# Final rows stored into the output and added to by scatters, a place per tile, VectorE roots and per-tile first weights in a routed transformer layer

## The chip, the cores and the metric

The kernel runs on one core of one Trainium2 chip. The metric is the device time of one execution in microseconds (us). Engines are named as the profile names them: PE (matmul), PEld (its weight loads), DVE (VectorE), ACT (ScalarE), POOL (GpSimd), SP (SyncE, which here only issues DMAs).

## The reference

x is 4 x 1024 x 256 in float32, 4096 tokens in all. LN is the layer norm without scale over the 256 channels.

```python
x = x + attention(LN(x)) @ w_proj.T     # causal, ALiBi slopes, 16 heads of 16
u = LN(x)
# attention over the first axis: each of the 1024 positions attends over the batch of 4
a = attention_over_batch(u @ in_proj_w.T + in_proj_b) @ out_w.T + out_b
h = LN(u + a) * ln1_g + ln1_b
probs = softmax(h @ router_w.T + router_b)          # 8 experts
assign = max(top_k(probs, 2).indices)               # the larger index of the best two
moe = gelu(h @ w1[assign].T + b1[assign]) @ w2[assign].T + b2[assign]
out = x + LN(h + moe) * ln2_g + ln2_b
```

Each token goes through one expert, number 1 to 7 (the larger of two different indices is never 0).

## The kernel before, in words

`kernel` lays the weights out and launches `tile_layer` (L2470), which runs `fast_layer` (L607 to 2467) and, under a flag that is not set here, a general fallback `general_layer` (L93). PE, DVE and ACT are called through a helper that records what they are given (`Watched`, L579), so in the profile nearly all their instructions stand at line 589 and are told apart by the names of their tiles. POOL and SP show their own lines.

The work comes in these stages:

- **Causal attention** in rounds of `score` and `weigh` (L986 to 1070), whose probabilities are masked by POOL (L1017). It fills some 600 us.
- **Fronts.** `front(i)` (L1593 to 1855) takes block i of 128 positions with all 4 of the batch, 512 tokens. It normalises x into u, projects q, k, v (`qkvp`), does the 4-way attention on DVE (`pr`, `sc`, `pv`), turns the result round with PE (`turned_sum`, L1724), projects, normalises h, and scores the router. Two rows per token are then stored by SP in one DRAM table `rows` of 4096 x 512: h normalised but not yet scaled (`rows<-u`, L1787 on) and x + ln2_b (`rows<-x`, `store_later`, L1613). There are 8 fronts; the earlier ones run inside the attention, the last one in the tail beside the first tiles.
- **Tables.** A tile is 128 tokens of one expert. `tabulate_first` (L1299) sorts the tokens of the first 6 fronts into 18 tiles (0_0 to 0_17), `tabulate_rest` (L1346) those left over and the last two fronts into 20 tiles (1_0 on). For each tile they find which rows to gather (`rows_`), where in the output they belong (`out_rows`), the expert's offset into the weights (`at_w`) and its one-hot row (`chosen`). The last 4 of the 20 run only under a condition that is not met here, so 34 tiles run.
- **Tiles** (class `Tile`, L1858). `gather` (L1865): POOL fetches 128 rows of 512 by an indirect DMA into a buffer `given`. `stages` (L1905): PE transposes h (`mtp`); ACT scales it by ln1 into `mt`; PE makes `hid` = w1 x mt + b1; ACT takes gelu (`ge`); PE sums `oe` = b2 + h (a matmul of `mt` with the identity) + w2 x ge. In the profile w1 and w2 are both `w`.
- **Pairs of tiles** are finished together by `finish_tiles` (L1961): DVE takes mean and variance from `oe`, POOL the root by a power (`norm_root`, L827, `rstd_v`), DVE makes (oe - mean) x ln2_g and then x rstd + (x + ln2_b) into `o` (4 buffers), and POOL scatters `o` into the output by an indirect DMA (`out_dram`, L1983) after a small memset (L1982).

w1 of all seven experts is loaded into SBUF by SP at the start of the tail (`load_layer`), and w2 a little later (`of_late`). The first 4 tiles load their own w1 and w2 (`load_weights`, L1874). For all others ACT copies the expert's w1 out of the resident one into one of 3 buffers (`copy_w1`, L1891), because its offset is a register's value; w2 is read in place.

**What sets the order.** Each engine takes its instructions in program order, and that order is written by a planner in Python. Generators such as `front` yield the engine and the cost of their next part (`yield "E", 2.0` is 2.0 us of DVE); the loop at L2417 takes whichever can begin first, and puts a tile's step (`tile_step`, L2415) in where PE would be free. A tile's costs are in `TILE` (L71). `Experts` (L1993) holds the tiles in flight: `fetch` takes a new one if one of the 18 `given` buffers is free (the pair that held it is finished), `advance` moves each tile in flight a stage on. 5 tiles of the first table are held back (`HELD_BACK`) to be issued around and after the second table. After `tabulate_rest`, `late["wide"]` is set: from there on only tiles are left, and `oe` has more buffers. The check of the attention's sums (`check_sums`, L2366) goes in at the eighth step after that, and its flag decides on the fallback.

Of the kernel before, what the change touches and what calls it, by code (L numbers as in the profile page):

```python
# [58 lines left out]
STEEP = -400.0  # L59
MASKED = -1e30  # L60
# [4 lines left out]
EARLY = 0  # L65
N_OWN = 4
N_GIVEN = 18
N_W1 = 3
HELD_BACK = 5

TILE = (("PE", 2.6), ("DVE", 1.7), ("ACT", 1.9), ("POOL", 2.3))  # L71
TILE_HALF, LAG, COPIED, FIRST_BY, W1_THERE, LOAD_W2 = 1.3, 0.2, 1.0, 0.1, 14.0, 2.0
# [535 lines left out]
def fast_layer(ctx: ExitStack, tc: tile.TileContext, odd, x, wq, wk, wv, wp, w_in, w_out, w_r,  # L608
# [222 lines left out]

    def norm_apply(dst, src, n, mv, rstd, name, scalar=False):
# [352 lines left out]
    given = [const(f"given{n}", [P, 2 * C]) for n in range(EARLY)]  # L1185
# [4 lines left out]
    def prepare():  # L1190
        nc.vector.tensor_scalar(lower, mask, -1.0, None, ALU.is_lt)
        nc.vector.memset(ones_bf, 1.0)
        nc.vector.memset(one_e, 1.0)
        for t in b_bf + [in_bf, out_bf]:
            nc.vector.memset(t, 0.0)
        for t in given:
            nc.gpsimd.memset(t, 0.0)

    class Routing:
# [6 lines left out]
        def prepare(self):  # L1206
            self.so_far = const("so_far", [P, E], BF16)
            nc.vector.memset(self.so_far, 0.0)
            self.rows_of = dram.tile([N_COLUMNS * P, 2 * C], F32, tag="rows", name="rows")
# [384 lines left out]
    def front(i, fact, more, last):  # L1594
# [3 lines left out]
        rows_of = part.rows_of.rearrange("(k t p) c -> k p t c", t=B, p=P)[i]  # L1598
        yield "E", 2.5
# [13 lines left out]
        def store_later():  # L1613
            for t in range(B):
                nc.sync.dma_start(rows_of[:, t, C:2 * C], at_x(t))
            left_x[i // PC] += 1
# [101 lines left out]
        if last:  # L1718
# [5 lines left out]
            def turned_sum(t, pr):  # L1724
                pt = bank(f"ctp_{i}_{t}")[:, :C].rearrange("p (c q) -> p c q", q=P)
                for cc in range(CC):
                    for k in range(B // 2):
                        nc.tensor.matmul(
                            pt[:, cc], pr[:, k, cc * P:(cc + 1) * P], ident,
                            start=k == 0, stop=k == B // 2 - 1,  # L1730
# [4 lines left out]
            for t in range(B):  # L1735
                yield "E", 2.0, 1.0 if t else 0.0
# [3 lines left out]
                nc.vector.tensor_tensor(pr[:, 0:2], pr[:, 0:2], pr[:, 2:4], ALU.add)  # L1740
# [49 lines left out]
        store(("u", i), lambda: nc.sync.dma_start(rows_of[:, :, 0:C], u))  # L1790
# [67 lines left out]
    class Tile:  # L1858


        def __init__(self, table, j):
            self.table, self.j, self.name = table, j, f"{table.n}_{j}"
            self.w1 = self.w2 = None
# [10 lines left out]
        def load_weights(self):  # L1874
# [6 lines left out]
            self.w1, self.w2 = (  # L1881
                const(f"{name}_{self.name}", [P, CC, C], into=late["tail"])
                for name in ("w1", "w2")
            )
            for t, src in ((self.w1, w1), (self.w2, w2)):
                nc.sync.dma_start(
                    t.rearrange("p c f -> p (c f)"),
                    src.rearrange("p e c f -> p (e c f)")[:, bass.ds(at + CC * C, CC * C)],
                )

        def copy_w1(self):  # L1891

            at = nc.values_load(
                self.table.at_w[0:1, self.j:self.j + 1], engines=[mybir.EngineType.Activation],
                min_val=0, max_val=(E - 2) * CC * C,
                skip_runtime_bounds_check_because="an expert is 1 to E - 1",
            )
# [63 lines left out]
    def finish_tiles(two):  # L1961

        n, name = len(two), two[0].name
        mv, rstd = norm_stats(lambda k: two[k].v, n, f"v_{name}", "_v")
        norm_root(rstd, n)
        yield
        if experts.waiting():
            yield
        os = []
        for k, t in enumerate(two):  # L1970
            o = late["work"].tile([P, C], F32, tag="o", name=f"o_{t.name}", bufs=4)
            nc.vector.scalar_tensor_tensor(
                o, t.v, mv[:, k, 0:1], row(G2), ALU.subtract, ALU.mult
            )
            nc.vector.scalar_tensor_tensor(
                o, o, rstd[:, k:k + 1], t.hx[:, C:2 * C], ALU.mult, ALU.add
            )
            os.append(o)
        if experts.waiting():
            yield  # L1980
        for t, o in zip(two, os):
# [4 lines left out]
                in_=o, in_offset=None, bounds_check=B * T - 1, oob_is_err=False,  # L1986
# [6 lines left out]
    class Experts:  # L1993
# [559 lines left out]
```

## Time and profile before

| what | value |
|---|---|
| median of 3 runs | 774.32 us (772.24 to 775.04) |
| the profiled execution | 776.72 us |
| its span | 774.9 us |
| granted PE clock, mean | 0.97 |
| PE busy | 696.7 us (90% of the span) |
| DVE, ACT, POOL busy | 514.0, 425.9, 243.0 us |
| gathers (POOL L1868) | 34, 1100 ns each |
| scatters (POOL L1983) | 34, 1018 ns each |
| last PE instruction ends | 759.2 us |

Times in the profile are microseconds from the start of the span; 1.8 us of the execution lie outside it. A row of a timeline gives start, duration, engine, line and operation, then the tiles written <- read with their shapes, how many records are joined (x4), and in brackets how long the engine was idle before it and what ended that. A row of the waits gives engine, tile and line of the waiting instruction <- what released it: the total of idle us, how often, the longest. A row of the stretches gives its window and length, then the busy us of PE, PEld, DVE, ACT and POOL, the granted PE clock, the busy share of the DMA engines and GB/s. An f32 matmul leaves two records, a transpose or a bf16 matmul one. "issue" is idle time for which the profile shows no release.

### The profile page before, as it was taken

What the parts mean: (1) busy time and instruction counts of PE and PEld (TensorE: products, weight loads), DVE (VectorE), ACT (ScalarE), POOL (GpSimd) and SP (SyncE); (2) the same over time, 40 slices, a digit from 0 to 9 for tenths busy, and PEclk for the clock granted to TensorE, in tenths of its full rate; (3) what the DMA queues carried; (4) which work ended last, traced back from release to release, by engine and by line L of the source; (5) the groups of instructions that cost most, each with busy time, mean ns of one, the idle gap of its engine ahead of it and who ended that gap; (6) DMA issues with size and microseconds to landing.
All of it is one profiled execution on the core that took longest, in us unless ns stands there. A gap on an engine that the chain in (4) does not pass through costs nothing. (4 is left out here: it accounts for less than half of the span.)

```text
span 774.9 us, 21884 instructions
## 1 busy us (share of the span) xinstructions
PE 696.7 (90%) x8945; PEld 525.6 (68%) x8945; DVE 514.0 (66%) x1266; ACT 425.9 (55%) x647; POOL 243.0 (31%) x345
## 2 busy tenths in 40 slices
PE   3989899999999999999989999999999687989991
PEld 2667577666666666575668877687778456878891
DVE  5447436477985765899672427698679778877462
ACT  1545547555465656556557656568558054546550
POOL 4644113221222221104221221123112330478873
PEclk9999999999999999999999999999999898999996
DMA  7535544431452432315354445345342670344421
GB/s 227 167 117 176 172 129 139 139 118 49 129 160 86 140 113 67 102 58 159 93 172 134 142 146 164 93 139 187 112 116 58 174 282 1 110 137 128 125 82 41
DMA packets 70872, 98.48 MB, mean 127 GB/s; under 512 B 15408, under 2 KB 54635, under 8 KB 70252
## 3 DMA queue, kind: packets, MB, share of 16 engines
q1 hardware_dynamic: 58528, 67.82, 28.4%
q10 hardware_dynamic: 7884, 16.05, 6.6%
q0 software_dynamic: 4352, 13.11, 5.6%
q8 instruction: 74, 1.21, 0.6%
q14 instruction: 34, 0.28, 0.1%
HBM read 60.50 MB, written 34.59 MB: 123 GB/s over the span
## 5 line engine op out<-in xcount | busy, mean ns | idle before, releaser
L589 ACT ACTIVATE p<-sk 128x1024 f32<-128x1024 f32 (+1 forms) x320 | 287.9, 940 | 148.4 <-PE sk L589 118.6
L1017 POOL TENSOR_SCALAR_AFFINE_SELECT p<-p 128x512 f32<-128x512 f32 (+1 forms) x160 | 106.6, 670 | 404.8 <-ACT p L589 402.5
L589 PE MATMUL sk<-slots 32*128 32x128 f32 (+1 forms) x3456 | 178.5, 325 | 10.1 <-DVE kq L589 4.7
L589 PEld LDWEIGHTS sk<-slots 32*128 32x128 f32 x3456 | 134.6, 187 | 53.5 <-issue 20.5
L589 PE MATMUL pv<-p,v 128*32 128x128 f32 (+1 forms) x3456 | 146.9, 317 | 9.6 <-ACT p L589 4.0
L589 PEld LDWEIGHTS pv<-p,v 128*32 128x32 f32 x3456 | 96.9, 111 | 48.8 <-issue 10.0
L589 PE MATMUL qkvp<-w_in,ut 128*128 128x264 f32 (+1 forms) x240 | 83.5, 486 | 0.2 <-ACT ut L589 0.2
L589 PEld LDWEIGHTS qkvp<-w_in,ut 128*128 128x128 f32 x240 | 42.5, 190 | 28.8 <-issue 24.3
L589 PE MATMUL qkp<-xt,wqk 128*128 128x256 f32 x224 | 56.4, 397 | 0.0
L589 DVE COPY kq<-qkp 128x512 f32<-128x512 f32 x28 | 19.1, 684 | 50.1 <-PE qkp L589 50.1
L589 PEld LDWEIGHTS qkp<-xt,wqk 128*128 128x128 f32 x224 | 41.5, 194 | 10.7 <-issue 3.3
L589 PE MATMUL hid<-mt,w 128*128 128x128 f32 x272 | 41.4, 289 | 2.6 <-ACT ge L589 1.7
L589 ACT ACTIVATE mt<-mtp,columns 128x128 f32<-128x128 f32 x68 | 27.4, 454 | 26.9 <-PE mtp L589 26.9
L589 ACT COPY qkv<-qkvp 128x512 f32<-128x512 f32 x28 | 16.4, 585 | 44.9 <-PE qkvp L589 44.7
L589 DVE TENSOR_TENSOR pv<-vr,sc 128x1024 f32<-128x1024 f32 x32 | 39.2, 1224 | 2.4 <-PE ctp L589 2.1
L1868 POOL DMA_INDIRECT given<-rows,rows x34 | 37.4, 1100 | 9.0 <-issue 7.9
L589 DVE COPY vr<-qkvp 128x264 f32<-128x264 f32 x28 | 12.1, 431 | 42.1 <-PE qkvp L589 42.1
L589 PEld LDWEIGHTS hid<-mt,w 128*128 128x128 f32 x272 | 37.2, 198 | 3.9 <-ACT ge L589 2.2
L589 DVE TENSOR_REDUCE sc<-pr 128x64 f32<-128x1024 f32 x32 | 39.0, 1220 | 1.1
L589 DVE TENSOR_TENSOR pr<-qkv 128x1024 f32<-128x1024 f32 x32 | 39.2, 1224 | 0.5 <-ACT qkv L589 0.2
L1983 POOL DMA_INDIRECT out_dram<-o,out_rows x34 | 34.6, 1018 | 7.4 <-issue 5.0
L589 PE MATMUL oe<-w,ge 128*128 (+1 forms) x136 | 36.8, 395 | 0.0
(320 smaller groups left out, 1005.1 us busy)
## 6 DMA issues: line engine op xcount, KB each, us to landing
slots<-k SPq DMA_DIRECT2D x32, 320.0 KB
k<-kq SPq DMA_DIRECT2D x32, 256.0 KB
v<-v ACTq DMA_DIRECT2D x4, 1152.0 KB
x<-in_x_dram SPq DMA_DIRECT2D x16, 256.0 KB
y<-yt SPq DMA_DIRECT2D x16, 256.0 KB
rows<-x SPq DMA_DIRECT2D x32, 128.0 KB
slots<-k SPq DMA_DIRECT2D x16, 256.0 KB
rows<-u SPq DMA_DIRECT2D x8, 512.0 KB
```

The costliest lines, as they stand in the source:

```text
L589: ins = made(*args, **kwargs)
L1017: nc.gpsimd.affine_select(blocks, blocks, pattern=[[0, 2], [0, size], [1, P]], compare_op=ALU.is_ge, fill=0.0, base=0, channel_multiplier=-1,)
L1868: nc.gpsimd.indirect_dma_start(out=self.hx, out_offset=None, in_=t.rows_of, in_offset=bass.IndirectOffsetOnAxis(ap=t.rows_[:, self.j:self. ...
L1983: ins = nc.gpsimd.indirect_dma_start(out=out.rearrange("t n c -> (t n) c"), out_offset=bass.IndirectOffsetOnAxis(ap=t.table.out_rows[:, t. ...
```

## The change

- Where x + ln2_b was stored into the table, it is stored straight into the output. The table has only h: 4096 x 256, and a gather brings 256 numbers per row.
- The scatters add (`compute_op=ALU.add`) what LN(h + moe) x ln2_g gives to the rows that lie in the output. The product is made in the tile's own gathered row: DVE's (oe - mean) x ln2_g overwrites `given`, ACT scales it there by rstd, and POOL scatters it from there. `o` and the second DVE operation are gone.
- Each tile has a place of its own in `given` (19 pairs); `fetch` no longer waits for a finished one.
- Behind the table (`wide`) the root is taken by DVE: a first guess by integer arithmetic and three Newton steps on 128 x 2 numbers, 12 small operations in `norm_root_v`. Ahead of it POOL still does it.
- w1 is not kept in SBUF. Each tile's w1 (256 KB) comes from DRAM by SP, with the offset in a register of SP, into one of 8 buffers. w2 is loaded first, and always read in place. ACT's copies are gone.
- In `turned_sum` of the last front, PE transposes and sums four parts where DVE first added them to two and PE multiplied two by the identity. In `oe` the identity's product becomes a transpose and comes ahead of the bias.
- The planner's numbers follow: `TILE`, a yield of the last front (2.0 to 1.3), when tiles may begin.

The parts of the diff that matter:

```diff
@@ -57,19 +57,18 @@
 N_LAST = 4
 NOWHERE = 1 << 20
+GUESS = float(0x5F3759DF - 0x00400000)
...
-EARLY = 0
-N_OWN = 4
-N_GIVEN = 18
-N_W1 = 3
+N_AHEAD = 4
+N_W1 = 8
...
-TILE = (("PE", 2.6), ("DVE", 1.7), ("ACT", 1.9), ("POOL", 2.3))
-TILE_HALF, LAG, COPIED, FIRST_BY, W1_THERE, LOAD_W2 = 1.3, 0.2, 1.0, 0.1, 14.0, 2.0
+TILE = (("PE", 2.5), ("DVE", 1.2), ("ACT", 1.7), ("POOL", 2.6))
+TILE_HALF, LAG, COPIED, FIRST_BY, W2_THERE = 1.3, 0.2, 1.0, 0.1, 2.0
...
@@ -829,6 +828,26 @@
+    def norm_root_v(mv, rstd, n):
+        half = small.tile([P, 2], F32, tag="half_v", name="half_v")[:, :n]
+        y = small.tile([P, 2], F32, tag="root_v", name="root_v")[:, :n]
+        by = rstd[:, :n]
+        nc.vector.tensor_scalar(half, mv[:, :n, 1], EPS, 0.5, ALU.add, ALU.mult)
+        nc.vector.tensor_single_scalar(
+            y.bitcast(I32), half.bitcast(I32), 1, op=ALU.logical_shift_right
+        )
+        nc.vector.tensor_scalar(
+            y.bitcast(I32), y.bitcast(I32), -1.0, GUESS, ALU.mult, ALU.add
+        )
+        for k in range(3):
+            nc.vector.tensor_tensor(by, y, y, ALU.mult)
+            nc.vector.scalar_tensor_tensor(by, by, -1.0, half, ALU.mult, ALU.mult)
+            nc.vector.scalar_tensor_tensor(
+                by if k == 2 else y, by, 1.5, y, ALU.add, ALU.mult
+            )
...
@@ -1206,7 +1223,7 @@
-            self.rows_of = dram.tile([N_COLUMNS * P, 2 * C], F32, tag="rows", name="rows")
+            self.rows_of = dram.tile([N_COLUMNS * P, C], F32, tag="rows", name="rows")
...
@@ -1596,6 +1613,8 @@
+
+        out_of = out.rearrange("t (k p) c -> k p t c", p=P)[i]
...
@@ -1612,7 +1631,7 @@
-                nc.sync.dma_start(rows_of[:, t, C:2 * C], at_x(t))
+                nc.sync.dma_start(out_of[:, t], at_x(t))
...
@@ -1723,21 +1742,21 @@
             def turned_sum(t, pr):
                 pt = bank(f"ctp_{i}_{t}")[:, :C].rearrange("p (c q) -> p c q", q=P)
+
                 for cc in range(CC):
-                    for k in range(B // 2):
+                    for k in range(B):
                         nc.tensor.matmul(
                             pt[:, cc], pr[:, k, cc * P:(cc + 1) * P], ident,
-                            start=k == 0, stop=k == B // 2 - 1,
+                            is_transpose=True, start=k == 0, stop=k == B - 1,
                         )
                 nc.scalar.copy(ct[:, :, t * P:(t + 1) * P], pt)
             pr = None
             for t in range(B):
-                yield "E", 2.0, 1.0 if t else 0.0
+                yield "E", 1.3, 1.0 if t else 0.0
                 if t:
                     turned_sum(t - 1, pr)
                 pr = weighted(t)
-                nc.vector.tensor_tensor(pr[:, 0:2], pr[:, 0:2], pr[:, 2:4], ALU.add)
             yield "D", 1.0
             turned_sum(B - 1, pr)
             for t in range(B):
...
@@ -1878,28 +1897,12 @@
                 min_val=0, max_val=(E - 2) * CC * C,
                 skip_runtime_bounds_check_because="an expert is 1 to E - 1",
             )
-            self.w1, self.w2 = (
-                const(f"{name}_{self.name}", [P, CC, C], into=late["tail"])
-                for name in ("w1", "w2")
-            )
-            for t, src in ((self.w1, w1), (self.w2, w2)):
-                nc.sync.dma_start(
-                    t.rearrange("p c f -> p (c f)"),
-                    src.rearrange("p e c f -> p (e c f)")[:, bass.ds(at + CC * C, CC * C)],
-                )
-
-        def copy_w1(self):
-
-            at = nc.values_load(
-                self.table.at_w[0:1, self.j:self.j + 1], engines=[mybir.EngineType.Activation],
-                min_val=0, max_val=(E - 2) * CC * C,
-                skip_runtime_bounds_check_because="an expert is 1 to E - 1",
-            )
             self.w1 = late["work"].tile(
                 [P, CC, C], F32, tag="w1", name=f"w1_{self.name}", bufs=N_W1
             )
-            nc.scalar.copy(
-                self.w1.rearrange("p c f -> p (c f)"), late["w1"][:, bass.ds(at, CC * C)]
+            nc.sync.dma_start(
+                self.w1.rearrange("p c f -> p (c f)"),
+                w1.rearrange("p e c f -> p (e c f)")[:, bass.ds(at + CC * C, CC * C)],
             )
         def stages(self):
...
@@ -1915,15 +1918,12 @@
                     mt[:, cc], pt[:, cc], AF.Identity,
                     bias=columns[:, 1, cc:cc + 1], scale=columns[:, 0, cc:cc + 1],
                 )
-            if not self.w1:
-                self.copy_w1()
             yield
-            if not self.w2:
-                at = nc.values_load(
-                    self.table.at_w[0:1, j:j + 1], engines=[mybir.EngineType.PE],
-                    min_val=0, max_val=(E - 2) * CC * C,
-                    skip_runtime_bounds_check_because="an expert is 1 to E - 1",
-                )
+            at = nc.values_load(
+                self.table.at_w[0:1, j:j + 1], engines=[mybir.EngineType.PE],
+                min_val=0, max_val=(E - 2) * CC * C,
+                skip_runtime_bounds_check_because="an expert is 1 to E - 1",
+            )
...
@@ -1946,44 +1946,48 @@
-            nc.tensor.matmul(self.v, sel, b_bf[1], start=True, stop=False)
+
             for cc in range(CC):
                 nc.tensor.matmul(
-                    self.v[:, cc * P:(cc + 1) * P], mt[:, cc], ident, start=False, stop=False
-                )
+                    self.v[:, cc * P:(cc + 1) * P], mt[:, cc], ident,
+                    is_transpose=True, start=cc == 0, stop=False,
+                )
+            nc.tensor.matmul(self.v, sel, b_bf[1], start=False, stop=False)
             for fc in range(CC):
                 nc.tensor.matmul(
                     self.v, ge[:, fc],
-                    self.w2[:, fc] if self.w2 else late["w2"][:, bass.ds(at + fc * C, C)],
+                    late["w2"][:, bass.ds(at + fc * C, C)],
                     start=False, stop=fc == CC - 1,
                 )
     def finish_tiles(two):
-        n, name = len(two), two[0].name
-        mv, rstd = norm_stats(lambda k: two[k].v, n, f"v_{name}", "_v")
-        norm_root(rstd, n)
+        n = len(two)
+        tiles = norm_tiles(f"v_{two[0].name}", "_v")
+        _, mv, rstd = tiles
+        for k, t in enumerate(two):
+            norm_one(tiles, k, t.v)
+
+            nc.vector.scalar_tensor_tensor(
+                t.hx, t.v, mv[:, k, 0:1], row(G2), ALU.subtract, ALU.mult
+            )
+        if late["wide"]:
+            norm_root_v(mv, rstd, n)
+        else:
+            norm_end(tiles, n)
+            norm_root(rstd, n)
         yield
+        for k, t in enumerate(two):
+            nc.scalar.activation(t.hx, t.hx, AF.Identity, scale=rstd[:, k:k + 1])
         if experts.waiting():
             yield
-        os = []
-        for k, t in enumerate(two):
-            o = late["work"].tile([P, C], F32, tag="o", name=f"o_{t.name}", bufs=4)
-            nc.vector.scalar_tensor_tensor(
-                o, t.v, mv[:, k, 0:1], row(G2), ALU.subtract, ALU.mult
-            )
-            nc.vector.scalar_tensor_tensor(
-                o, o, rstd[:, k:k + 1], t.hx[:, C:2 * C], ALU.mult, ALU.add
-            )
-            os.append(o)
-        if experts.waiting():
-            yield
-        for t, o in zip(two, os):
+        for t in two:
             nc.gpsimd.memset(spare, 0.0)
             ins = nc.gpsimd.indirect_dma_start(
                 out=out.rearrange("t n c -> (t n) c"),
                 out_offset=bass.IndirectOffsetOnAxis(ap=t.table.out_rows[:, t.j:t.j + 1], axis=0),
-                in_=o, in_offset=None, bounds_check=B * T - 1, oob_is_err=False,
+                in_=t.hx, in_offset=None, bounds_check=B * T - 1, oob_is_err=False,
+                compute_op=ALU.add,
             )
             if late["n_out"]:
                 tc.declare_no_dep(ins.ins, group="rows", reason="a token is in one tile")
...
@@ -1996,30 +2000,27 @@
         def __init__(self):
             self.step, self.fetched = 0, []
-            self.n_fetched = self.n_finished = 0
+            self.n_fetched = 0
             self.under_way, self.done, self.finishing = [], [], []
         def fetch(self):
             self.step += 1
-            if tiles_to_do and self.n_fetched - self.n_finished < len(given):
+            if tiles_to_do and given:
                 t = tiles_to_do.pop(0)
-                t.gather(given[self.n_fetched % len(given)])
-                if self.n_fetched < N_OWN:
-                    t.load_weights()
+                t.gather(given[self.n_fetched])
+                t.load_weights()
                 self.n_fetched += 1
                 self.fetched.append((t, self.step))
         def finish(self):
             for it in list(self.finishing):
-                n, stages = it
-                if next(stages, self) is self:
+                if next(it, self) is self:
                     self.finishing.remove(it)
-                    self.n_finished += n
             n = 1 if len(self.done) + len(self.under_way) + self.waiting() < 2 else 2
             if len(self.done) >= n:
                 two, self.done = self.done[:n], self.done[n:]
-                self.finishing.append((len(two), finish_tiles(two)))
-                next(self.finishing[-1][1])
+                self.finishing.append(finish_tiles(two))
+                next(self.finishing[-1])
...
@@ -2037,10 +2038,6 @@
-            if self.fetched and self.n_fetched > 2 * N_OWN + 1:
-                t, _ = self.fetched[0]
-                if not t.w1:
-                    t.copy_w1()
...
@@ -2330,32 +2327,31 @@
     issue_stores(age=0)
-    load_sums(last_unit)
...
-    w1_sb, w2_sb = (const(name, [P, E - 1, CC, C], into=tail) for name in ("w1", "w2"))
-
-    def load_layer(sb, src):
-        for lo, hi in ((1, 3), (3, 5), (5, E)):
-            nc.sync.dma_start(sb[:, lo - 1:hi - 1], src[:, lo:hi])
+    w2_sb = const("w2", [P, E - 1, CC, C], into=tail)
+    for lo, hi in ((1, 3), (3, 5), (5, E)):
+        nc.sync.dma_start(w2_sb[:, lo - 1:hi - 1], w2[:, lo:hi])
     late.update(
         tail=tail, work=work, ps=ps_x, wide=False, n_oe=0, n_out=0, n_hid=0,
-        w1=w1_sb.rearrange("p e c f -> p (e c f)"), w2=w2_sb.rearrange("p e c f -> p (e c f)"),
+        w2=w2_sb.rearrange("p e c f -> p (e c f)"),
     )
-    for k in range(EARLY, N_GIVEN):
-        if k < EARLY + X_BUFS - B - G // 2:
-            given.append(xpool.tile([P, 2 * C], F32, tag="x", name=f"given{k}"))
+
+    for k in range(N_TILES // 2):
+        if k < X_BUFS - B - G // 2:
+            two = xpool.tile([P, 2, C], F32, tag="x", name=f"given{k}")
         else:
-            given.append(const(f"given{k}", [P, 2 * C], into=tail))
-    for _ in range(N_OWN):
+            two = const(f"given{k}", [P, 2, C], into=tail)
+        given += [two[:, 0], two[:, 1]]
+    for _ in range(N_AHEAD):
         experts.fetch()
     fetching.clear()
-    load_layer(w1_sb, w1)
+    load_sums(last_unit)
     running += [Running(it) for it in queue]
     queue.clear()
...
@@ -2410,7 +2404,7 @@
-        return max(free["PE"], W1_THERE if experts.n_fetched > 2 * N_OWN else 0.0)
+        return max(free["PE"], W2_THERE)
```

More of the change, by code (lines that the diff above doesn't have):

```diff
@@ L1184, in fast_layer @@
     out_bf = const("out_bf", [P, C + E], BF16)
-    given = [const(f"given{n}", [P, 2 * C]) for n in range(EARLY)]
+    given = []
     row_no = numbered("row_no", [P, 1], [[0, 1]], up=1)
@@ L1195, in prepare @@
             nc.vector.memset(t, 0.0)
-        for t in given:
-            nc.gpsimd.memset(t, 0.0)
     class Routing:
@@ L1788, in front @@
         )
-        store(("u", i), lambda: nc.sync.dma_start(rows_of[:, :, 0:C], u))
+        store(("u", i), lambda: nc.sync.dma_start(rows_of, u))
         key = small.tile([P, B, E], F32, tag="key", name=f"key_{i}", bufs=2)
@@ L1862, in __init__ @@
             self.table, self.j, self.name = table, j, f"{table.n}_{j}"
-            self.w1 = self.w2 = None
+            self.w1 = None
         def gather(self, hx):
@@ L2373, in check_sums @@
         )
-    of_late = [(LOAD_W2, lambda: load_layer(w2_sb, w2))]
     late["at_place"] = ends.tile([P, 2 * B, P], BF16, tag="su", name="at_places", bufs=2)
@@ L2423, in fast_layer @@
     while threads:
-        for at, what in list(of_late):
-            if free["PE"] >= at:
-                of_late.remove((at, what))
-                what()
         at, _, it = min((begin(it) + FIRST_BY * n, n, it) for n, it in enumerate(threads))
```

## The prediction

> **What bounds the kernel now.** The first two thirds are attention, with PE busy 90% of the span; the instruction order of the changed kernel is the same there up to about 605 us. So I read the busy time by stretches of the tail, then the waits from 680 on, then one period of each engine's timeline, then the end of the chain.
>
> ```profile
> 634.00:683.00 49.00, 41.75 (x295) 36.37 (x294) 42.02 (x103) 27.14 (x59) 13.89 (x16) 0.93 0.22 67
> 683.00:701.00 18.00, 13.20 (x108) 11.96 (x104) 12.73 (x46) 7.22 (x16) 14.06 (x20) 0.91 0.43 133
> 701.00:742.00 41.00, 38.63 (x301) 35.82 (x300) 23.67 (x68) 25.30 (x56) 35.13 (x48) 1.00 0.42 126
> 742.00:760.00 18.00, 17.19 (x132) 15.68 (x130) 12.11 (x35) 8.19 (x19) 13.56 (x24) 1.00 0.18 61
> ```
>
> Columns: length, then busy PE, PEld, DVE, ACT, POOL, the granted clock, DMA share, GB/s. Until the second table (about 683) DVE is full, 42.0 of 49. From 701 PE is at 94% and POOL at 86%: two engines near their ends, and DVE has 17 us to spare. Between them, 683 to 701, PE has a hole.
>
> ```profile
> DVE o L589 <- DMA out_dram<-o,out_rows: 9.2, 6, 3.2
> DVE o L589 <- POOL rstd_v L828: 8.2, 8, 1.5
> PE oe L589 <- DVE stats_v L589: 7.2, 4, 3.5
> ```
>
> DVE's two waits (17.4 us) are what the change removes: for a buffer `o` that a scatter still reads, and for POOL's root. Neither is PE's. PE's own wait is the third: it can't start an oe while DVE, at work on the table, hasn't read the older sums.
>
> ```profile
> 706.22 0.73 POOL L828 TENSOR_TENSOR rstd_v<-rstd_v,minus_half 128x2 f32<-128x2 f32 x1
> 707.14 1.28 POOL L1868 DMA_INDIRECT given<-rows,rows  x1 [0.19 <-PE mtp L589]
> 708.41 0.13 POOL L1982 MEMSET spare<- 128x1 f32 x1
> 708.72 1.02 POOL L1983 DMA_INDIRECT out_dram<-o,out_rows  x1 [0.18 <-issue]
> ...
> 710.05 1.00 POOL L1983 DMA_INDIRECT out_dram<-o,out_rows  x1 [0.19 <-issue]
> 711.36 1.06 POOL L1868 DMA_INDIRECT given<-rows,rows  x1 [0.30 <-issue]
> 712.43 0.75 POOL L828 TENSOR_TENSOR rstd_v<-rstd_v,minus_half 128x2 f32<-128x2 f32 x1
> ```
>
> A pair of tiles takes POOL 6.2 us (706.22 to 712.43): root, two gathers, two scatters of 1.31 with their memset and gap. Without the root it is 5.3.
>
> ```profile
> 678.06 0.17 DVE L589 TENSOR_SCALAR whole<-whole 128x4 int32<-128x4 int32 x1
> 678.26 0.17 DVE L589 CAST by<-whole 128x4 f32<-128x4 int32 x1
> 678.47 0.16 DVE L589 SCALAR_TENSOR_TENSOR left<-by,rank 128x4 f32<-128x4 f32 x1
> ...
> 686.95 0.42 DVE L589 BATCH_NORM_STATS2 stats_v<-oe 128x6 f32<-128x256 f32 x1
> ```
>
> A tiny DVE operation that needs the one before it starts 0.20 to 0.21 us after it.
>
> ```profile
> 691.14 0.27 PE L589 MATMUL oe<-b_bf,chosen 128*128 128x256 bf16 x1 [3.47 <-DVE stats_v L589]
> ...
> 703.81 0.38 PE L589 MATMUL mtp<-ident,given 128*128 128x128 f32 x2
> ...
> 705.19 0.61 PE L589 MATMUL oe<-ident,mt 128*128 128x128 f32 x4
> 705.64 1.03 PE L589 MATMUL oe<-w,ge 128*128 x4
> 706.50 0.38 PE L589 MATMUL mtp<-ident,given 128*128 128x128 f32 x2
> ```
>
> A tile costs PE 2.70 us. Its four identity records advance PE by 0.45. After the 3.47 us stall the four w records took 1.92 in place of 1.03.
>
> ```profile
> 763.52 0.99 POOL out_dram L1983
> ```
>
> The chain ends here: the last oe ends at 759.19, the last scatter starts 4.33 later, and the span ends 11.4 us after its start (774.9). The profiled execution is 776.72 (1.8 outside the span), 2.4 above the median 774.32; I sum on the profile and scale by 774.32/776.72.
>
> **Before the second table: -5.3 us of lead.** The last block's four adds (128x512, 0.69 each, 2.8 us) leave DVE; PE turns four parts in place of two sums, with no more records, because a transpose needs one where the f32 product needs two. Each finished tile has one scaled add less (0.40 us of DVE's time); some six tiles fall into the stretch: 2.4. DVE is 86% full, so both arrive nearly whole: the table begins at about 671.6 where it began at 676.97, and DVE starts on the waiting pair at about 681.8 where it did at 686.95. Storing x into `out` takes the places of the stores into `rows`; all four last ones go out at about 660, the first scatter comes at about 667. I cost that at nothing; if a store landed late, the first scatter and the gathers behind it on POOL would wait as long.
>
> **The new wait behind the table: +5.9.** After the table the root is 12 dependent DVE operations: 12 x 0.20 = 2.4 us in place of POOL's 0.73. A pair costs DVE 2 x (0.46 + 0.21 + 0.40) + 2.4 = 4.5. Three pairs are queued at 681.8, so DVE is behind until 681.8 + 3 x 4.55 = 695.5. ACT's order in the changed kernel has each pair's two scalings ahead of the next mt, so mt, ge and with them PE's hid wait for DVE's root: PE gets about one tile per 4.5 us and is idle some 4 between, as at 691.14, at the slower clock. With 1.6 for scaling and mt and 0.35 to the matmul, hid of the 14th tile comes at about 697.5; it came at 697.03. The lead is spent.
>
> Here a rule must be weighed. The Trainium skill ("VectorE: DVE Perf Modes", the section on the TRN2 errata) has a table by which an SBUF operation costs 58 cycles plus its length at 0.96 GHz: 62 ns for these, 0.75 us per root, 2.9 per pair; then there would be no backlog. The same section says that the measured fixed term is about 150 cycles (156 ns). The rows above say 200 ns with the dependence; I take them.
>
> **The steady part: -4.5, with +1.9 once.** PE loses 0.22 per tile (two identity records), 2.70 to 2.48. The copy of w1 on ACT (0.62) goes and one scaling comes (0.4 to 0.5 by half of a 128x256 ACTIVATE pair): even. But the order makes a loop: the pair's last oe, DVE 3.5 (statistics, product, root), ACT 0.8 + 0.81 (scalings, mt) and 0.35 (ge), then PE 4.74 for hid, oe, mtp, hid, oe: 10.5 us for two pairs, 5.25 per pair. PE alone would give 4.96, DVE 4.55. From the 14th tile to the last it was 58.9 us for 20 steps, 2.94 each (5.9 a pair). 20 x 2.625 = 52.5, and the last oe ends at 697.5 + 52.5 + 4.2 = 754.2. The check of sums, some 1.9 us of DVE, now lies on the loop: 756.1.
>
> **First weights.** 256 KB per tile come by SP. SP waits for a free one of eight buffers with only later weights behind it. Gathers halve to 128 KB, so bytes per tile go from about 384 KB to 640 with the scatter's reading: some 240 GB/s at 2.6 us a tile, over the 126 of the row, under the 282 that one slice of the page reached. A tile is fetched some 10 us ahead, the gather lands in 3.3. Hidden; if not, each lateness is PE's.
>
> **Scatters.** The profile has no accumulating scatter. The nearest row is the plain one, 1.0 us of POOL, 2.5 to land. Below nothing is excluded[...]. The skill ("DMA: Bandwidth & Descriptors", Rules for kernel authors) says that an accumulate reads its destination and writes it later; it gives no price. I take +0.2 of POOL each (bounds 0 and 1.0), and +1.0 of landing (0.3 to 2). After 686.5 POOL has 30 x 1.31 + 15 x 1.35 = 59.6 us: it is done by 752 with that, inside the loop's end.
>
> **The end.** The last oe to the last scatter: statistics and product 1.1, root 2.4, scaling 0.5, first scatter and gap 1.4, some 0.2 of hand-overs: 5.6 where it was 4.3. 756.1 + 5.6 = 761.7, against 763.52: -1.8; with 1.0 of landing -0.8. Sum: 776.7 - 0.8 = 775.9 at the profile, with 0.5 to 1 of the small gains on PE before the table left over, 775.3; scaled 773.
>
> **Rivals.** *Slower: the accumulating scatter fills POOL.* POOL's end is 745 + 30d for the last scatter's start, d being the extra per scatter. It passes 761.7 at d = 0.55, is slower by over 0.5% from about 0.74, and at d = 1.0 ends 13 us later: 785. For it: POOL is at 86% already.[...] *Faster: no backlog.* If ACT's scalings don't hold mt up, or the small operations run at 0.06, PE runs on at 4.96 to 5.0 a pair from about 679: 62.7 us to 742, scatters end by 748: 757. Halfway, with the backlog but a loop bound by PE (4.96): 10 pairs x 0.29 and part of the lead, 768. *A longer loop.* If scaling or hand-overs add 0.3 per half turn, 10 pairs x 0.3 and the lost clock: 778 to 780.
>
> **Numbers.** No measurable difference is within 0.5% (3.9 us), about what a measurement of this kernel can tell. My case, 771 to 777: 0.38, of which 0.34 stay within. Halfway faster 0.18, no backlog 0.12; POOL 0.20; longer loop 0.12, nearly all slower. That gives faster 0.32, same 0.34, slower 0.34. The likeliest is 773; for 8 in 10 the range takes in the halfway case and most of POOL's: 762 to 785.
>
> **What would show it.** Rank near 671.6; DVE's root chain 2.4 us long and PE waiting between 683 and 697 behind ACT's scalings; hid of the 14th tile near 697.5; pairs 5.25 apart; the scatter's row near 1.2; the end 11 to 13 us after the last scatter's start. Wrong if the scatter row is over 1.5, if PE has no hole at 685 to 695, or if oe waits for first weights.

## The result, and the profile after

The changed kernel takes 785.01 us (median of 4 runs, 782.96 to 786.35) against 773.7 us before: 1.0144 times, 95% interval 1.0111 to 1.0177. I had forecast 773.0 with a range up to 785.0, so the time lies just past its upper end. The profiled execution is 782.96 us, with a span of 781.2. On the chips of the experiments the kernel before itself took 783 to 786 us, and on the one where the changed kernel ran beside it the change cost less (1.0052). So experiments are read as ratios within one chip, and as distances inside one trace.

The same stretches of the tail as before the change, then its waits from 680 us on:

```profile
683.00:701.00 18.00, 14.21 (x76) 11.72 (x77) 12.18 (x56) 8.90 (x23) 14.56 (x17) 0.81 0.60 113
701.00:742.00 41.00, 36.27 (x255) 31.53 (x254) 29.49 (x125) 19.58 (x51) 35.09 (x39) 0.96 0.72 157
742.00:760.00 18.00, 15.73 (x113) 13.26 (x111) 12.84 (x57) 8.39 (x22) 10.53 (x14) 1.00 0.34 39
760.00:782.00 22.00, 0.78 (x4) 0.35 (x2) 4.71 (x23) 1.81 (x4) 6.58 (x7) 0.58 0.24 29
```

```profile
ACT given L588 <- DVE rstd_v L588: 36.7, 15, 5.3
DVE stats_v L588 <- PE oe L588: 14.8, 9, 4.3
...
POOL out_dram L1986 <- ACT given L588: 12.9, 9, 2.7
PE mtp L588 <- ACT mt L588: 11.0, 6, 3.8
```

PE lost its 94% between 701 and 742: it has 36.3 of 41 us, at a granted clock of 0.96, and it now waits for ACT's mt. ACT in turn waits 36.7 us for DVE's root, and DVE 14.8 us for PE's oe. None of the three is busy all the time, and each waits for the next: a loop. It can be followed around once in the timeline of all engines, the rows of one turn picked out:

```profile
726.97 0.43 DVE L588 BATCH_NORM_STATS2 stats_v<-oe 128x6 f32<-128x256 f32 x1 [2.17 <-PE oe L588]
...
731.38 0.16 DVE L588 SCALAR_TENSOR_TENSOR rstd_v<-rstd_v,root_v 128x2 f32<-128x2 f32 x1
731.58 0.91 ACT L588 ACTIVATE given<-given,rstd_v 128x256 f32<-128x256 f32 x2 [2.81 <-DVE rstd_v L588]
...
732.40 0.79 ACT L588 ACTIVATE mt<-mtp,columns 128x128 f32<-128x128 f32 x2
...
733.23 0.44 PE L588 MATMUL mtp<-ident,given 128*128 128x128 f32 x2 [1.27 <-ACT mt L588]
...
735.21 1.03 PE L588 MATMUL oe<-w,ge 128*128 x4
```

The next statistics but one start at 738.75. So a turn for two pairs is 11.8 us: 4.6 on DVE, 1.7 on ACT, 5.5 on PE. The starts of statistics before and after give the same (715.17, 726.97, 738.75, 750.51). That is 5.9 us per pair, just what a pair took before the change.

POOL's own queue is full until its gathers are out: from 689 to 742 us it never waits more than 0.31 us. The row of the page, one pair of the timeline, and the end of the chain:

```profile
L1986 POOL DMA_INDIRECT out_dram<-given,out_rows x34 | 54.0, 1587 | 17.7 <-ACT given L588 12.9
```

```profile
727.14 1.62 POOL L1986 DMA_INDIRECT out_dram<-given,out_rows  x1 [0.19 <-issue]
728.19 0.68 POOL L1985 MEMSET spare<- 128x1 f32 x1
729.06 1.60 POOL L1986 DMA_INDIRECT out_dram<-given,out_rows  x1 [0.19 <-issue]
730.96 1.08 POOL L1887 DMA_INDIRECT given<-rows,rows  x1 [0.30 <-issue]
732.35 1.04 POOL L1887 DMA_INDIRECT given<-rows,rows  x1 [0.31 <-issue]
```

```profile
768.13 1.56 DMA out_dram<-given,out_rows
```

An adding scatter costs POOL 1.59 us where a plain one cost 1.02, and takes 4.1 us to land (2.5 before). The last one starts at 768.13, 7.35 us after the last oe ended (760.78), and the span ends 13.1 us later.

### The profile page after: what moved, and what is told of

The parts are those of the page before. It is cut to its first block, busy times and chain, and to the rows that moved or that the text cites. A ratio compares the mean times of both kernels' runs of the same rounds, so it can differ in the third digit from the quotient of the medians.

```text
span 781.2 us, 22006 instructions
## 1 busy us (share of the span) xinstructions
PE 694.9 (89%) x8877; PEld 520.0 (67%) x8877; DVE 526.0 (67%) x1393; ACT 420.8 (54%) x651; POOL 252.0 (32%) x330
## 5 line engine op out<-in xcount | busy, mean ns | idle before, releaser
L1986 POOL DMA_INDIRECT out_dram<-given,out_rows x34 | 54.0, 1587 | 17.7 <-ACT given L588 12.9
L588 PE MATMUL hid<-mt,w 128*128 128x128 f32 x272 | 44.7, 304 | 3.7 <-ACT ge L588 2.7
L588 PEld LDWEIGHTS hid<-mt,w 128*128 128x128 f32 x272 | 39.0, 207 | 7.5 <-ACT ge L588 6.9
L588 ACT ACTIVATE given<-given,rstd_v 128x256 f32<-128x256 f32 x34 | 15.4, 500 | 40.7 <-DVE rstd_v L588 36.7
L588 PE MATMUL oe<-w,ge 128*128 x136 | 36.9, 396 | 0.0
```

The lines of the kernel that those rows point to most:

```text
L588: ins = made(*args, **kwargs)
L1986: ins = nc.gpsimd.indirect_dma_start(out=out.rearrange("t n c -> (t n) c"), out_offset=bass.IndirectOffsetOnAxis(ap=t.table.out_rows[:, t. ...
```

## Where the 11 us came from

The start of the tail differs between executions by some microseconds for reasons that lie in the attention (DVE's first reading of the seventh block's ao comes at 615.84 us in the changed kernel's profile, at 619.55 in the other, and anywhere from 616.9 to 622.0 in the experiments). So I count from that ao. "Table" is the second table's last offset `at_w`.

| stretch | before | after | change | forecast |
|---|---|---|---|---|
| first ao of block 7 to table | 67.3 | 62.8 | -4.5 | -5.3 |
| table to hid of the 14th tile | 10.2 | 15.9 | +5.8 | +5.9 |
| that hid to the end of the last oe | 62.2 | 66.2 | +4.1 | -3.6 |
| last oe to the start of the last scatter | 4.3 | 7.4 | +3.0 | +1.3 |
| last scatter's start to the end | 11.4 | 13.1 | +1.7 | +1.0 |

The sum is +10.0 us. The first two rows are as forecast. The third row is where it went wrong.

One trace of each kernel carries some 3 us of chance: in a second pair, the runs e9 (before) and e5 (after) below, on two other chips, the five changes are -3.7, +4.9, -0.6, +3.3 and +1.9 us, +5.8 in all (e9 has two short stalls in the third stretch, told of below). So the third row is not surely a loss of 4 us. What both pairs show is that the forecast gain of 3.6 us is not there.

## The experiments

**Theory A**: the loop of latency sets the pace behind the table. **Theory B**: POOL's dearer scatters set it. All distances below are from the runs' own traces; in the profiles shown above they were 72.3 and 4.3 us before the change, 82.2 and 7.3 after it.

| kernel | ratio to before, same chip | table to last oe | last oe to last scatter |
|---|---|---|---|
| before (e9) | 0.9985 (0.9961 to 1.0009) | 75.3 | 4.3 |
| changed (e5) | 1.0052 (1.0027 to 1.0076) | 79.6 | 7.6 |
| scalings later (e1) | 0.9917 (0.9882 to 0.9953) | 69.7 | 11.1 |
| scalings later (e12) | 0.9969 (0.9939 to 0.9998) | 69.3 | 11.4 |
| scalings later (e15) | 0.9973 (0.9954 to 0.9992) | 69.3 | 11.4 |
| two banks (e2) | 0.9983 (0.9961 to 1.0005) | 77.3 | 7.1 |
| two Newton steps (e3) | 0.9957 (0.9935 to 0.9979) | 78.2 | 6.8 |
| all three (e6) | 0.9990 (0.9971 to 1.0010) | 74.2 | 7.0 |
| plain scatters (e4) | 1.0129 (1.0053 to 1.0206) | 90.5 | 6.9 |
| scalings later, plain scatters (e13) | 1.0050 (1.0022 to 1.0078) | 76.6 | 8.4 |
| POOL's root (e11) | 1.0130 (1.0060 to 1.0200) | 87.5 | 7.5 |
| before, DVE's root (e7) | 1.0257 (1.0201 to 1.0313) | 88.2 | 8.0 |
| before, w1 from DRAM (e10) | 1.0029 (1.0003 to 1.0055) | 77.4 | 4.2 |
| before, PE's two edits (e8) | 0.9935 (0.9910 to 0.9960) | 73.1 | 4.3 |
| before, PE's two edits (e14) | 0.9942 (0.9916 to 0.9968) | 72.2 | 4.4 |

**ACT's scalings one step later (e1, again as e12 and e15).**

```diff
         yield
+        if late["wide"] and experts.waiting():
+            yield
         for k, t in enumerate(two):
             nc.scalar.activation(t.hx, t.hx, AF.Identity, scale=rstd[:, k:k + 1])
-        if experts.waiting():
+        if not late["wide"] and experts.waiting():
             yield
```

> Changed kernel, with ACT's two scalings of a pair put one tile's step later behind the table (behind the next mt and ge instead of ahead of them); nothing else moves. Theory A (a loop of latency: last oe of a pair, DVE statistics and root, ACT scaling, then the mt that stands behind it, PE for two tiles; 11.8 us for two pairs in the changed kernel's profile) expects the loop to shrink to about 9.3 us for two pairs, under PE's own 9.9: PE's waits for mt (11.0 us) nearly vanish, hid of the 14th tile comes before 690, the last oe ends 6 to 9 us earlier, and the time falls to 776 to 780. Theory B (POOL's accumulating scatters, 1.59 in place of 1.02 us, fill POOL from 689 to 741 and set the end) expects PE to be earlier but the last scatter to move by less than 1 us: 784 to 786.

> The changed kernel with ACT's scalings one tile's step later, again, now beside a trace of the kernel before on the same chip. Expected 0.988 to 0.999 of the kernel before, its last oe 68 to 72 us behind the table and its last scatter 9 to 12 us after that, POOL being the bound.

> The changed kernel with ACT's scalings one tile's step later, once more. Expected 0.990 to 0.999 of the kernel before, and 0 to 4 us slower than the kernel before with PE's two edits: POOL ends it at 80.8 us behind the table, where plain scatters and POOL's root end at 77 to 79.

The loop is gone: the last oe ends 69 to 70 us behind the table where it was 80, earlier than in the kernel before. In e12 a turn of two pairs falls to 10.0 us (statistics start at 721.35 and at 731.33), and PE waits for ACT's mt only three times, all before 702 us:

```profile
PE mtp L588 <- ACT mt L588: 4.7, 3, 1.8
```

Nothing was taken away or made faster; two scalings of each pair only stand elsewhere in ACT's order. That shows A for PE. The last scatter moved too, from 87.2 us behind the table to 80.8, where B allowed less than 1 us. But the time of e1, 781.6, lies between what A and B said, and the last scatter comes 11 us after the last oe. POOL's timeline of e12 says why:

```profile
752.24 1.56 POOL L1988 DMA_INDIRECT out_dram<-given,out_rows  x1 [0.19 <-issue]
753.21 0.70 POOL L1987 MEMSET spare<- 128x1 f32 x1
754.10 1.56 POOL L1988 DMA_INDIRECT out_dram<-given,out_rows  x1 [0.19 <-issue]
755.07 0.71 POOL L1987 MEMSET spare<- 128x1 f32 x1
755.97 1.56 POOL L1988 DMA_INDIRECT out_dram<-given,out_rows  x1 [0.19 <-DVE root_v L588]
```

Scatter follows scatter 1.87 us apart with nothing awaited; PE is done at 755.7 and POOL at 768.7. So once the loop is gone B holds, and the gain that is left against the changed kernel's 1.0052 (on another chip) is 0.8 to 1.3%.

**The pair's two oe in two banks (e2).**

```diff
-            late["n_oe"] += 1
+            late["n_oe"] += 2 if late["wide"] and late["alone"] else 1
+            late["alone"] = late["alone"] and not late["wide"]
```

> Changed kernel, with the first tile behind the table alone in its PSUM bank of oe, so that the two tiles of a finished pair lie in two banks, as they did before the change (in the changed kernel a pair shares a bank, and DVE's first statistics start only at the end of the second oe). Theory A, with this as a part of its loop, expects the first tile's statistics and product (1.07 us) to be over when the second oe ends: 10.7 in place of 11.8 us for two pairs, five turns, and 1.07 at the end: 5 to 6.5 us less, 778 to 780. Theory B expects no change, 784 to 786.

**Two Newton steps (e3).**

```diff
-        for k in range(3):
+        for k in range(2):
...
-                by if k == 2 else y, by, 1.5, y, ALU.add, ALU.mult
+                by if k == 1 else y, by, 1.5, y, ALU.add, ALU.mult
```

> Changed kernel with two Newton steps in place of three: 9 small DVE operations in place of 12, 0.59 us less per pair; the root is then right to about 5e-6. Theory A expects 1.2 us less in each turn of two pairs, some 6 us less from the 14th tile on, and 0.6 at the end: 777 to 780. Theory B: DVE has 10 us to spare between 711 and 757, so nothing, 784 to 786.

As ratios both are below the control, by 0.7 and 0.95%, about what A said (0.6 to 1.0%), and B expected nothing. But the control ran on another chip than these two, and from the table to the last oe they take only 2.3 and 1.4 us less than it, under half of what A said and no more than two traces of one kernel differ. So the totals leave A's sizes open, and what counts is inside the traces. In e2 a pair's first statistics no longer wait for its second oe:

```profile
745.26 0.42 DVE L588 BATCH_NORM_STATS2 stats_v<-oe 128x6 f32<-128x256 f32 x1
...
746.07 1.03 PE L588 MATMUL oe<-w,ge 128*128 x4
```

A turn in the middle of its tail is 10.7 to 11.2 us, where the control's is 11.8 to 12.3; the forecast was 10.7. Part of this is lost again right behind the table, where the hid of the 14th tile comes 17.1 us after it (15.9 in the control). In e3 that hid comes 13.9 us after the table: the backlog of four pairs is 2.0 us shorter, about four times 0.59. Its later turns are uneven (11 to 14 us), so a gain per turn can't be read off.

**The control (e5) and all three cuts (e6).**

> The changed kernel itself, beside the kernel before on one chip and beside the three below. Both theories expect 1.011 to 1.018 times the kernel before, as it was measured first; its table of the second stage is done 62 to 68 us after the first ao of the seventh block, its last oe ends some 82 us after that (72.3 in the kernel before).

> Changed kernel with all three cuts at once: ACT's scalings one tile's step later behind the table, the pair's two oe in two banks, two Newton steps. With the scalings moved alone, the last oe ended 70 us behind the table in place of 82, but the last scatter started only 11 us after it, POOL being busy without a gap for 75 us. Theory B for what is left (POOL's adding scatters, 1.87 us apart in place of 1.31, are the bound once the loop is gone) expects that the other two cuts change nothing: the last scatter within 1 us of that of the moved scalings, and the time 0.99 to 0.995 of the changed kernel. Theory A alone expects PE to go on setting the end: the last scatter within 7 us of the last oe, some 4 us less than the moved scalings alone.

In the control the ratio is 1.0052, below the 1.011 that I expected: on this chip, where the kernel before is slower, the change cost less; why is not shown. The three cuts together bring the last scatter to 81.1 us behind the table; the later scalings alone gave 80.8, 80.7 and 80.7. That is B's expectation for what is left, and so is the time, 0.994 of the changed kernel on the same chip. A's sign, a last scatter within 7 us of the last oe, came too (7.0), but only because the last oe is later here (74.2). One thing I had not foreseen: with the pair in two banks, PE waits right after the table until DVE frees one:

```profile
PE oe L588 <- DVE given L588: 9.2, 5, 6.6
```

**Plain scatters (e4), and plain scatters with later scalings (e13).**

```diff
                 in_=t.hx, in_offset=None, bounds_check=B * T - 1, oob_is_err=False,
-                compute_op=ALU.add,
             )
```

> Changed kernel with plain scatters in place of the adding ones; it leaves out the addition of x + ln2_b, the rest stands. Theory A expects the loop to stay at 11.8 us for two pairs, and the end to gain what one scatter (0.57) and the landing (1.6) cost: 782 to 783.5. Theory B expects POOL's pair to fall from 6.55 to 5.4 us and with it 8 to 11 us: 774 to 777.

> The changed kernel with ACT's scalings one tile's step later and plain scatters in place of adding ones; it leaves out the addition of x + ln2_b. If POOL's adding scatters hold the end once the loop is gone, the scatter takes 1.0 us, POOL gets gaps, the last scatter starts 6 to 7 us after the last oe in place of 11, and 76 us after the table in place of 80.8; if something else holds it, the 11 us stay. Alone, plain scatters came with a slower kernel, in which ACT, DVE and SP stood still together several times; such stalls would make the total time unreadable, not the distance from the last oe to the last scatter.

The scatter took 1.0 us, so the addition itself is what costs POOL 0.57:

```profile
L1986 POOL DMA_INDIRECT out_dram<-given,out_rows x34 | 34.5, 1013 | 46.1 <-ACT given L588 41.0
```

The total answered neither theory: e4 became 1.3% slower. In its trace ACT and DVE stand still for 2 to 7 us, several times, and the profile names no instruction that released them ("remote"):

```profile
ACT ge L588 <- remote: 12.2, 3, 7.1
...
DVE stats_v L588 <- remote: 4.3, 1, 4.3
```

What these stalls are I could not find out. The semaphore awaited in each of them is the one that PE's matmuls move. In e7 it does not move between 704.25 and 710.69 us and then four times within 0.3 us, though the profile, which models the ends of matmuls, has four of those that move it end between 704.9 and 707.6. So it is PE's signals that come late; whether PE itself stood still is not shown. Such stalls also come, shorter, in e1, e7, e9, e10, e11 and e13, not in the two first profiles.

In e13 POOL does get its gaps (it waits 28.7 us for ACT's scalings, 5.5 in e12), and the last scatter comes 8.4 us after the last oe where it was 11.4; 6 to 7 were expected. But PE's last oe is 7 us later than in e12, which by itself gives POOL time, so e13 agrees with B without proving it; the expected 76 us from the table were 85.0. That POOL is held by its scatters rests on the rows of e12 above and on e6.

**POOL's root again (e11).**

```diff
-        if late["wide"]:
-            norm_root_v(mv, rstd, n)
-        else:
-            norm_end(tiles, n)
-            norm_root(rstd, n)
+        norm_end(tiles, n)
+        norm_root(rstd, n)
```

> Changed kernel with the root behind the table on POOL again (one addition on DVE, then POOL's power), the rest as it is. If DVE's root were the whole of the loss, this would win it back: 0.985 to 1.0 of the kernel before. My theory says that POOL, with its scatters 1.87 us apart, has no room for it: a pair costs POOL 6.55 + 0.75 + 0.2, and ACT's scaling, with mt behind it, then waits for POOL's queue instead: 7.5 us per pair in place of 5.9 for ten pairs, 12 to 20 us slower than the changed kernel, 1.02 to 1.03 of the kernel before.

Now ACT's scaling waits for POOL, and mt behind it for that:

```profile
ACT given L588 <- POOL rstd_v L827: 43.6, 15, 6.9
```

A pair takes 7.2 us (7.5 expected), and the ratio is 1.013: 0.8% above the control, less than the 12 us or more that I expected. From the table to the last oe it is 87.5 us, where the control has 79.6. So the loss is not DVE's root alone: with adding scatters on POOL, the root costs more there than on DVE.

**Before, with DVE's root only (e7).**

```diff
-        norm_root(rstd, n)
+        if late["wide"]:
+            norm_root_v(mv, rstd, n)
+        else:
+            norm_root(rstd, n)
```

> Kernel before, with only the root behind the table moved from POOL to DVE (three Newton steps, 12 small operations). Here no ACT instruction waits for the root, and DVE takes both o operations after it. Theory A (the root is dear because ACT's scaling, and mt behind it, wait for it) expects little: DVE needs 2 x 1.47 + 2.4 = 5.3 us per pair, just under PE's 5.4, POOL falls from 6.2 to 5.3; between -3 and +4 us, 1.5 likeliest, with PE's waits for statistics a little longer. The rival (the small operations themselves are the cost: 2.4 us on each of 11 pairs while DVE is behind) expects +6 to +12 us.

This is a miss for me: 1.0257. From the table to the last scatter it is 96.1 us, where e9, on another chip, has 79.6: 16.5 more, of which 7.8 are two stalls of DVE of the unknown kind (e9 has one of 2.1). If they are simply taken off, the other 8.7 are in the rival's range (6 to 12). DVE's second product is still there, and PE waits 12.6 us for statistics (6.1 in e9). But DVE isn't full (48.0 of the 66 us from 694 to 760), and PE's granted clock in that stretch is 0.87 where e9 has 0.98. How much is the small operations, the stalls and the clock, this run does not separate.

**Before, with w1 from DRAM only (e10), and the kernel before itself (e9).** The edit is that of `load_weights`, `copy_w1` and the order of loading in the change.

> The kernel before itself, for its trace on the chip of the runs below; on the chips of the first experiments it took some 10 us more than where it was first measured. Expected 1.00; if the time lies in the attention, the first ao of the seventh block comes later than 619.6 us; if in the tail, the stretch from there to the end is longer than the 155.3 us of the first profile.

> Kernel before with one part of the change alone: w2 resident and loaded first, each tile's w1 from DRAM by SP into one of 8 buffers, ACT's copies gone; nothing else of the change. My prediction's step (hidden, costs nothing) expects 0.996 to 1.003. The rival (a load from DRAM that comes late makes PE wait for hid) expects PE's waits before hid to grow by 5 us or more and the time with them, 1.006 or more.

The table is equally far (70.6 and 70.7), the last oe 2.1 us later, the ratio at the edge of 1.003. PE waits 4.2 us ahead of hid (4.1 in e9), and none of it for w1. So the first weights are hidden from PE; whether they cost something elsewhere, this ratio is too close to 1 to tell. On this chip the kernel before has the same attention as at first (ao at 616.9), and its tail is 161.6 us long where it was 155.3: 3.3 of it up to the table and 3.0 from there to the last oe, where two stalls of the unknown kind lie (2.3 us of ACT, 2.1 of DVE).

**Before, with PE's two edits (e8, again as e14).** The edits are those of `turned_sum` (with its yield) and of the identity product in oe.

> Kernel before, with only the two edits on PE: the last block's four parts turned and summed by PE (four adds of 0.69 us less on DVE) and the identity product in oe as a transpose, ahead of the bias (0.22 us less per tile). Expected: the table some 3 us earlier, and 0.22 us on each of 20 tiles where PE is the bound, less what POOL's 6.2 us per pair take back: 3 to 7 us faster than the kernel before, 0.991 to 0.996.

> The kernel before with PE's sum of four turned parts and the transpose in oe, again, on one chip with the next. Expected 0.990 to 0.996 of the kernel before.

Both runs agree: 0.9935 and 0.9942. On the chip of the last runs this is 778.9 us, the kernel with later scalings 781.4 us, the kernel before 783.7 us. It beats the kernel before, and it is the part of the change that needed no new wait; its lead over the later scalings is small (the two intervals of the ratio overlap). The traces do not show where it gains: the table comes 69.1 and 70.2 us behind the ao (67.3 and 70.7 in the two traces of the kernel before), so the 3 us that I expected there can't be told from chance.

## Why the prediction was wrong

- **The lead before the table was right**: -4.5 for a forecast -5.3. (Rank came at 666.7 us, not 671.6; 3.7 of this is the earlier start of the tail. Counted from the ao it came 6.6 us earlier, but from there to the end of the table it took 11.9 us in place of 9.9, a loss that the sum had at nothing.)
- **The backlog behind the table was right**, in mechanism and size: four pairs (three in the sum) 4.4 to 4.8 us apart on DVE, ACT waiting for each root, PE idle 3.8 us and 1.7 us for it, +5.8 us for a forecast +5.9 (in the second pair of traces +4.9). The row of 0.20 us per small dependent operation held, too: 12 took 2.4 us. An estimate from the Trainium skill's 58 cycles ("VectorE: DVE Perf Modes", TRN2 errata) would have been 0.75, and one from its note of about 150 cycles 1.9; one operation lasts 0.16 us here, near that note, and 0.04 more pass before the next begins. PE's two holes and the wait of ACT between them:

```profile
684.93 0.56 PE L588 MATMUL mtp<-ident,given 128*128 128x128 f32 x2 [3.80 <-ACT mt L588]
...
692.40 0.91 ACT L588 ACTIVATE given<-given,rstd_v 128x256 f32<-128x256 f32 x2 [2.85 <-DVE rstd_v L588]
...
694.05 0.44 PE L588 MATMUL mtp<-ident,given 128*128 128x128 f32 x2 [1.72 <-ACT mt L588]
```

- **The steady part failed**, by 7.7 us. I had the loop, and it is what sets the pace, but its turn was mis-sized: I gave it 10.5 us for two pairs (the terms that I listed make only 10.2, and the -4.5 at the head of that paragraph is -5.5 by its own figures, which the total uses), a gain of 0.65 per pair; it was 11.8, which is no gain. Over ten pairs that is 6.5 of the 7.7 us; where the rest lies is not shown. Two terms were too small. DVE: 3.5 in the sum, 4.6 measured. I took the first tile's statistics and product as done when the second oe ends, which is so when the two lie in different PSUM banks, as they did before the change. In the changed kernel one tile fewer is issued ahead of the table, the pairs fall into one bank, and the first statistics wait for the bank's last matmul, that of the second oe. e2 showed the size: 0.6 to 1.1 per turn. PE: 4.7 in the sum, 5.5 measured. The turn starts with an mtp, which waits for mt because mtp has one place only, and the first records after each hole are slower (0.44 and 0.68 in place of 0.38 and 0.61).
- **The end** was too short by 1.7 us, mostly for the same reason: both tiles' statistics, product and root lie behind the last oe, and the first of the two scatters is 0.57 dearer.
- **The scatter was mis-sized**: +0.57 us of POOL against +0.2, +1.6 of landing against +1.0. My slower rival said that POOL decides from +0.55 on. It was full until 742 but was not what held PE: from there to the end POOL waits for ACT, not the reverse. It became the bound as soon as the loop was taken out (e1, e12, e15). A scatter's row over 1.5 was one of the prediction's own signs of being wrong, and it came.
- First weights hidden: right, as far as e10 can tell. The gathers never made PE wait.

The likeliest case therefore missed by one loop that ran as slowly as the loop it replaced, with the backlog and the longer end on top. My "longer loop" rival, 778 to 780, was the right one, but too short and for another reason: it put the excess into scaling and hand-overs, and ACT's part was 1.7 us where the sum had 1.6. That the time lies so near the upper end of the range is luck: that end was there for the rival in which POOL decides, and POOL did not.

## What to carry to other kernels

When a step is handed to another engine, write down the whole turn of latency that it joins, and ask of each instruction in it whether it waits for one tile or for all that share its bank or buffer. An instruction put ahead of an independent one in the same queue makes this wait for whatever it waits for: two scalings per pair, moved by one step, were worth 10 us on PE. Look then for the engine that is next: here POOL's dearer scatters had been hidden behind the loop, and of the 10 us only 6.5 reached the last scatter.

## What was not expected of the hardware

- An adding indirect scatter of 128 rows of 1 KB costs POOL 1.59 us where the plain one costs 1.0 (e4 and e13 against the rest), and lands in 4.1 us where the plain one took 2.5. The memset behind it takes 0.69 in place of 0.12, beside the scatter.
- In 7 of the 17 profiles ACT or DVE waits 1 to 7 us, several times, for the semaphore that PE's matmuls move, after the profile has those matmuls as ended or without a record of them. The cause stays open.
